# A two-layer graph kernel: owner matrices turned on TensorE, limits compared on GpSimd, and a new order of issue

## Chip, cores and metric

The kernel runs on one core of one Trainium2 chip. The metric is device time in microseconds (us) of one execution, the median over runs; lower is better. The core has five engines that run beside each other: TensorE (PE in the profile, with its weight loads as PEld), VectorE (DVE), ScalarE (ACT), GpSimd (POOL) and SyncE (SP, which here only issues transfers). Each engine works through its own instructions strictly in the order in which the program issues them, and waits on semaphores for the others.

## The reference, cut to what matters

There are 128 graphs (B) of 128 nodes (N) with 64 features (F). Layer 0 has 192 hidden units (H). Its sum over neighbours of a relu of a pair is the costly part:

```
mask = (adj > 0)
h  = relu(x@W1a [j] + (x[j]-x[k])@W1b + b1)        # for every pair j,k
hm = einsum('bjkh,bjk->bjh', h, mask)
x  = layernorm(x + hm@W2 + deg*b2)                 # layer 0
m  = relu(relu(x@W1+b1)@W2+b2);  msg = relu(adj@m)
r,z,n = gates(msg@W_ih, x@W_hh)                    # a GRU cell
x  = layernorm(x + (1-z)*n + z*x)                  # layer 1
```

Roughly one pair in eight is an edge (an edge is drawn with a mean chance of 0.0625 in each direction and then made symmetric), and some nodes have many more than others. The kernel therefore does not compute all pairs: for each node it gathers the projected rows of its neighbours, one neighbour slot after another.

## The kernel before, in words

The graphs are worked on in 32 groups of four (G = 4). A group passes through parts, each a Python generator whose steps issue a few instructions:

- `load`: transfers of `adjT`, `xT` and `x`. All go through SP's queue; `adjT` and `xT` of group 0 go through ACT's.
- `masks`, `ranks`, `degrees`, `counts`: a 0/1 mask (GpSimd, L422), the rank of each neighbour by a triangular product (L429, copied to `rankT`, L432), the degrees (L437 to L442), and the number of extra segments of each node (`nseg`, GpSimd, L447 to L455).
- `offsets` (L458 to L478): where each node's extra segments begin. Two small products (`po`, L462), ACT copies one of them as `woff` (L465), VectorE compares a ramp with the other one straight from PSUM, which gives `till` (L470, one instruction of 128x512), TensorE turns `till` into the owner matrix `pp` (L473), and ACT copies that twice, as `own` (bf16, L476) and `own32` (f32, L478).
- `turned` (L487): `rankT` transposed by a DMA on SP's queue. `owners` (L493): `own` transposed in the same way into `ownTh`, which ACT widens to `ownT` (f32, L498). `places` (L500): the slot numbers of extra segments.
- `pick0`, `pick1`: 0/1 selection matrices, made on VectorE (L518, L532, L540). `pieces` and `values0`: the two projections (L547), one of them split into three bf16 pieces b0, b1, b2 (ACT L574, TensorE L577).
- `seed0`, `gather0`, `keep0`, `reduce`: the first neighbour slots of every node. ACT seeds a PSUM tile `pv` (L606), TensorE adds twelve products of selections and pieces (L636; one such gather is "x12" in the profile), ACT applies the first relu (L656) and VectorE adds the others (L666). `gather0[i,k]` stands below for graph i and step k. `over0`, `over2` (`pz`, L617, copied as `us`, L623), `seed1`, `gather1`, `keep1`, `reduce1` do the same for the extra segments of nodes with many neighbours.
- `base`, `together`, `joined` (GpSimd, L686 to L699) and `sums` (`ph`, L711 to L730) add everything up into `hmT`.
- `second` (L286): layer 0's last product (`pw`, L290 and L294), the sum `y` (VectorE, L298), and a layernorm: statistics on VectorE (L260, L262), four short steps on GpSimd (L265 to L271), and four ACT instructions that write `x1` (L275). `turn` transposes `x1` (`pt`, L305, copied as `x1T`, L309). Then come `message1` to `message3` (`pm`, `pn`, `pa`), `gates` (`pg`) and `update`, which ends in a second layernorm and the store.

Two pools of PSUM are shared by all parts: three tiles for `pv` and the pieces, and two tiles for everything else (`pc`, `pd`, `po`, `pp`, `ps`, `pu`, `pz`, `ph`, `pw`, `pt`, `pm`, `pn`, `pa`, `pg`), so that a product waits until the tile two places earlier has been read.

The order of all work is written out by hand. `TIMETABLE` gives each step of each part a key; group g's step has the key plus g times 100,000, and the program issues all steps of all groups in the order of their keys. So in the steady state every 100,000 keys make a period, in which each part of some group is issued once, and a key's last five digits (after adding 100,000 until it is positive) give its place in the period. `FIRST` and `SETUP` replace the keys of group 0 and of the constants, and the last group is finished in two halves of two graphs (parts named `_a` for the half that holds graphs 0 and 1). In this last group `filler(n)` issues n products of zeros on TensorE between the steps of its tail.

Of the kernel before, what the change touches and what calls it, by code (L numbers as in the profile page):

```python
# [8 lines left out]
F32 = mybir.dt.float32  # L9
BF16 = mybir.dt.bfloat16  # L10
I32 = mybir.dt.int32
AF = mybir.ActivationFunctionType
ALU = mybir.AluOpType
AX = mybir.AxisListType

N = 128
# [3 lines left out]
G = 4  # L20
# [8 lines left out]

PER = 100000  # L30
TIMETABLE = {
    "load": (-374155,), "masks": (-371858,), "ranks": (-359377, -359144), "degrees": (-369319, -367849),
    "turned": (-272568, -171369), "counts": (-333387,), "offsets": (-310900, -305943, -303488, -292051, -285534),
    "owners": (-153741, -131732), "places": (-270818, -268534),
    "pieces": (-333718, -314824, -313814, -310191, -307850, -307567, -306941, -306158, -304141, -301647, -297445),
    "others": (-209792, -151063), "values0": (-277700, -277635, -275480),
    "pick0": (-320732, -302387, -282581, -212470), "pick1": (-264046, -174794), "over0": (-187960, -184290),
    "over2": (-185520, -182217), "base0": (-167649,), "base1": (-162372,), "base2": (-164467,), "base3": (-167914,),
    "together0": (-192391, -176074, -152715), "sums0": (-135068, -121634, -119241, -112824), "joined0": (-123048,),
    "joined2": (-118176,), "together1": (-152595, -149638, -144598), "together2": (-138498, -136957, -119891),  # L40
    "sums2": (-106974, -105339, -103492, -102357), "together3": (-118393, -118393, -118207),
    "second": (-101830, -101830, -95538, -87073, -83594, -80961), "turn": (-71249, -69447),
    "message1": (-68165, -67985), "message2": (-66138, -64498), "message3": (-64168, -63125),
    "gates": (-61275, -60655, -60562, -60317, -60317, -59857),
    "update": (-28741, -17657, -15933, 2994, 5175, 17014, 40040, 59482, 73748),
    "second_a": (-111100, -110015, -107069, -106567, -103378, -99663), "turn_a": (-92426, -81714),
    "message1_a": (-77007, -70724), "message2_a": (-67059, -65898), "message3_a": (-64395, -63864),
    "gates_a": (-2585, 1906, 7556, 8397, 14259, 14787),
    "update_a": (31311, 98242, 403034, 540592, 1029378, 1397305, 1422534, 2329328, 3382657),
    "seed0": (-239029, -208652, -204666, -193414, -193414, -184279, -167332, -163359),  # L50
    "gather0": (-236595, -215481, -206970, -203094, -202533, -193838, -186392, -183598, -181405, -172481, -169740,
        -166341, -163928, -161205, -159527, -145074), "keep0": (-218713, -195286, -179448, -161724),
    "reduce": (-209107, -203867, -196740, -190891, -186219, -180588, -169406, -168830, -166160, -161020, -158388,
        -143709), "seed1": (-174669, -161027),
    "gather1": (-170052, -167751, -164502, -162019, -160643, -157628, -136154, -128967), "keep1": (-168203, -159725),
    "reduce1": (-166795, -164060, -161924, -149299, -134445, -118338),
}


LAST = ("second_a", "turn_a", "message1_a", "message2_a", "message3_a", "gates_a", "update_a")  # L60
SETUP = (-385974, -327363, -291126, -281259, -225667, -75165)
FIRST = {
    "load": (-287111, -272305), "masks": (-279478,), "ranks": (-272173, -266612), "degrees": (-258449, -257828),
    "turned": (-188322, -105244), "counts": (-244130,), "offsets": (-216625, -212945, -212777, -205972, -195707),
    "places": (-185210, -182042),
    "pieces": (-270553, -265591, -263742, -257675, -254043, -249305, -246306, -243488, -243290, -240054, -221265),
    "values0": (-244645, -244472, -237344), "pick0": (-236759, -233220, -233160, -207088),
    "pick1": (-177321, -171760), "over0": (-195488, -187431),
}


# [1 line left out]
def adj_resnorm_kernel(  # L73
# [19 lines left out]
    nc = tc.nc  # L93
# [6 lines left out]
    ident_h = const.tile([N, N], BF16, name="ident_h")  # L100
# [13 lines left out]
    iota = const.tile([N, N], BF16, name="iota")  # L114
# [24 lines left out]
    def each(t, n):  # L139

        return t.rearrange("p (o c) -> p o c", o=1).to_broadcast([t.shape[0], n, t.shape[1]])
# [95 lines left out]
    def wide(t, n, w=F):  # L237
        return t.rearrange("p (g o) -> p g o", o=1).to_broadcast([N, n, w])
# [10 lines left out]
    def tail_parts(g, work, ps_w, n, store, lo=0, fill=True):  # L249

        name = g["name"]
        s = {}
# [26 lines left out]
        def filler(n):  # L279

            if fill and name == str(ng - 1):
                p = g["spare"]
                for i in range(n):
                    nc.tensor.matmul(p, ones_h, zeros, start=True, stop=True)

        def second():  # L286
            ps = [ps_w.tile([N, n // 2, F], F32, tag="w", name=f"pw{name}") for h in range(2)]
            hm = g["hmT"]
            for i in range(n):
                nc.tensor.matmul(ps[i % 2][:, i // 2, :], hm[:, (lo + i) // 2, i % 2, :], w2c[:, 0, :], start=i < 2, stop=False)  # L290
            yield
            for i in range(n):
                hs = slice(i % 2 * F, (i % 2 + 1) * F)
                nc.tensor.matmul(ps[i % 2][:, i // 2, :], hm[hs, (lo + i) // 2, 2, :], w2c[hs, 1, :], start=False, stop=i >= n - 2)  # L294
            yield
            y = work.tile([N, n, F], F32, tag="y0", name=f"y0_{name}")
            for h in range(2):
                nc.vector.tensor_add(y[:, h:n:2, :], ps[h], g["t4"][:, lo + h : lo + n : 2, :])  # L298
            filler(9)
            yield from layernorm(y, "0", "x1")  # L300

        def turn():
# [87 lines left out]
    with ExitStack() as fast:  # L390
        loads = fast.enter_context(tc.tile_pool(name="loads", bufs=4))
        prep = fast.enter_context(tc.tile_pool(name="prep", bufs=2))
# [3 lines left out]
        ps_w = fast.enter_context(tc.tile_pool(name="ps_w", bufs=2, space=bass.MemoryType.PSUM))  # L396

        def loading(s):
            def part():
                g = s["g"]  # L400
                gs = slice(g * G, (g + 1) * G)
                s["adjT"] = loads.tile([N, G, N], F32, tag="adjT", name=f"adjT{g}")
                q = nc.scalar if g == 0 else nc.sync
                q.dma_start(s["adjT"], adjT[:, gs, :])
                if g == 0:
                    yield

                s["xT"] = loads.tile([N, 2, N], F32, tag="xT", name=f"xT{g}")
                for h in range(2):
                    q.dma_start(s["xT"][h * F : (h + 1) * F], xT[:, g * G + h : (g + 1) * G : 2, :])  # L410
                s["x"] = loads.tile([N, G, F], F32, tag="x", name=f"x{g}")
                nc.sync.dma_start(s["x"], x[:, gs, :])
                yield

            return part

        def prep_parts(s):
            g = s["g"]
# [39 lines left out]
            def offsets():  # L458

                p = ps_w.tile([N, 2, G], F32, tag="w", name=f"po{g}")  # L460
                for c, m in enumerate((strict, incl)):
                    nc.tensor.matmul(p[:, c, :], m, s["nseg"], start=True, stop=True)  # L462
                yield
                s["woff"] = prep.tile([N, G], BF16, tag="woff", name=f"woff{g}")
                nc.scalar.mul(s["woff"], p[:, 0, :], 2.0 * W1)  # L465
                yield


                s["till"] = prep.tile([N, G, N], BF16, tag="till", name=f"till{g}")
                nc.vector.tensor_tensor(s["till"], each(iota, G), wide(p[:, 1, :], G, N), ALU.is_lt)  # L470
                yield
                p = s["po"] = ps_w.tile([N, G, N], F32, tag="w", name=f"pp{g}")
                nc.tensor.matmul(p, step, s["till"], start=True, stop=True)  # L473
                yield
                s["own"] = prep.tile([N, G, N], BF16, tag="own", name=f"own{g}")
                nc.scalar.copy(s["own"], s["po"])  # L476
                s["own32"] = prep.tile([N, G, N], F32, tag="own32", name=f"own32_{g}")
                nc.scalar.copy(s["own32"], s["po"])  # L478
# [12 lines left out]
                yield  # L491

            def owners():  # L493
                t = prep.tile([N, G, N], BF16, tag="ownTh", name=f"ownTh{g}", bufs=1)
                nc.sync.dma_start_transpose(t, s["own"].rearrange("p g n -> p (g n)"))
                yield
                s["ownT"] = prep.tile([N, G, N], F32, tag="ownT", name=f"ownT{g}")
                nc.scalar.copy(s["ownT"], t)  # L498

            def places():  # L500

# [245 lines left out]
        name, g, run = "setup", -1, setup(ps_g, ps_w)  # L747
# [153 lines left out]
```

## Time and profile before

| what | value |
|---|---|
| time, median of 3 runs | 963.09 us (959.31 to 966.01) |
| the profiled execution's own time | 966.28 us |
| its span, first to last instruction | 964.5 us, granted clock of TensorE 0.988 |
| busy TensorE, VectorE, ScalarE, GpSimd | 899.8, 861.4, 834.4, 771.6 us |
| chain that ended last, by engine | PE 53%, ACT 25%, DVE 16%, issue 5% |
| first gather of group 0 | starts at 17.04 us |
| last add of the last group (L666) | ends at 936.61 us |

A line of a timeline gives start, duration, engine, source line, operation, tile written from tiles read, shape and count; neighbouring instructions of one kind are merged, and idle time ahead of it stands in brackets with what ended it. A line of a table by stretches gives, for each engine, its busy time and its number of instructions. Products on TensorE overlap, so that the time from one line's start to the next one's start says more than the duration in the line.

### The profile page before, as it was taken

How to read it: one execution, taken by the hardware profiler on the slowest of the kernel's cores; microseconds unless marked ns; L12 is line 12 of the kernel's file. 1: busy time of each engine (PE TensorE's matmuls, PEld its weight loads, DVE VectorE, ACT ScalarE, POOL GpSimd, SP SyncE). 2: the span in 40 equal slices, each digit the busy share in tenths (PEclk: the TensorE clock that was granted, in tenths of full speed). 3: DMA queues.
4: the chain of work that ended last, by engine and by line, in shares of the span. 5: the costliest groups of instructions: out<-in, count | busy, mean ns of one | idle time of the engine just before them, and what ended most of it. 6: DMA issues, size and time to landing. Idle time of an engine off the chain costs nothing.

```text
span 964.5 us, 32114 instructions
## 1 busy us (share of the span) xinstructions
PE 899.8 (93%) x13081; PEld 711.2 (74%) x13084; DVE 861.4 (89%) x1628; ACT 834.4 (87%) x1705; POOL 771.6 (80%) x1113
## 2 busy tenths in 40 slices
PE   6889999999999999999999999999999999999984
PEld 3667777777777777777777777777777777777762
DVE  7898999999999999999999999999999999999772
ACT  4778889999989989988999898998998899989763
POOL 4548888888988888988888898888898888888663
PEclk9999999999999999999999999999999999999997
DMA  3101110012111012111012111102111201110000
GB/s 104 46 3 33 40 40 19 24 40 40 41 40 33 10 41 40 40 40 39 11 32 40 40 40 41 30 12 40 39 41 40 41 9 34 40 40 19 13 7 14
DMA packets 60523, 32.27 MB, mean 33 GB/s; under 512 B 38989, under 2 KB 56275, under 8 KB 60371
## 3 DMA queue, kind: packets, MB, share of 16 engines
q1 hardware_dynamic: 59938, 29.78, 12.8%
q8 instruction: 104, 1.70, 0.7%
q10 hardware_dynamic: 432, 0.39, 0.1%
q14 instruction: 49, 0.39, 0.1%
HBM read 17.57 MB, written 4.19 MB: 23 GB/s over the span
## 4 chain that ended last, share of the span: by engine, by line
PE 53%; ACT 25%; DVE 16%; issue 5%; POOL 1%; ACTq 0%; DVEq 0%; POOLq 0%
PE pv L636 25%; DVE acc L666 10%; ACT pv L606 7%; PE ph L718 4%; ACT x L275 3%; PE pw L290 3%; PE pv L547 3%; ACT acc L656 3%; ACT b L574 3%; ACT us L623 3%; PE ph L724 2%; PE pw L294 2%; DVE n L362 2%; ACT own L476 2%; PE pm L313 2%
## 5 line engine op out<-in xcount | busy, mean ns | idle before, releaser
L666 DVE SCALAR_TENSOR_TENSOR acc<-pv,acc 128x768 f32<-128x768 f32 x576 | 536.2, 949 | 62.4 <-PE pv L636 46.7
L636 PE MATMUL pv<-b,pick 64*128 64x192 bf16 x9216 | 476.8, 244 | 42.3 <-DVE acc L666 17.0
L636 PEld LDWEIGHTS <-pick 64*128 64x128 bf16 x9216 | 383.8, 95 | 130.0 <-issue 106.0
L606 ACT COPY pv<-u 128x768 f32<-128x768 f32 x256 | 204.7, 805 | 2.8 <-DVE acc L666 2.1
L656 ACT ACTIVATE acc<-pv 128x768 f32<-128x768 f32 x192 | 154.1, 803 | 14.2 <-PE pv L636 11.4
L691 POOL TENSOR_TENSOR fs<-acc,nb 128x192 f32<-128x192 f32 x128 | 76.4, 597 | 106.2 <-ACT nb L678 101.3
L686 POOL TENSOR_TENSOR acc<-acc 128x384 f32<-128x384 f32 x128 | 128.0, 1000 | 25.3 <-DVE acc L666 25.3
L688 POOL TENSOR_TENSOR acc<-acc 128x192 f32<-128x192 f32 x128 | 130.7, 1021 | 5.1
L518 DVE TENSOR_TENSOR pick<-rankT,ramp 128x2048 bf16<-128x2048 bf16 x64 | 91.5, 1432 | 0.0
L574 ACT CAST b<-pv 128x384 bf16<-128x384 f32 x192 | 83.0, 487 | 9.1 <-PE pv L547 3.0
L269 POOL TENSOR_TENSOR rs<-ve,nhalf 128x4 f32<-128x4 f32 (+1 forms) x66 | 86.1, 1305 | 0.0
L699 POOL TENSOR_TENSOR acc<-acc 128x384 f32<-128x384 f32 x64 | 78.0, 1219 | 0.5 <-DVE acc L666 0.5
L606 ACT COPY pv<-us 128x768 f32<-128x768 f32 x64 | 51.9, 811 | 24.5 <-DVE acc L666 24.5
L730 ACT COPY hmT<-ph 128x384 f32<-128x384 f32 x64 | 30.6, 478 | 36.9 <-PE ph L724 36.9
L617 PE MATMUL pz<-u,own 128*128 128x192 f32 x256 | 58.3, 350 | 0.2 <-ACT us L623 0.2
L532 DVE TENSOR_TENSOR pick<-pick 128x1024 bf16<-128x1024 bf16 x64 | 56.4, 882 | 0.0
L678 ACT ACTIVATE nb<-u,npad 128x192 f32<-128x192 f32 x128 | 53.8, 445 | 0.0
L422 POOL TENSOR_SCALAR maskT<-adjT 128x512 bf16<-128x512 f32 x32 | 48.3, 1510 | 4.4 <-DMA adjT<-in_adjT_dram 4.4
L376 POOL TENSOR_TENSOR uc<-ub,tn 128x256 f32<-128x256 f32 x31 | 51.1, 1648 | 0.0
L275 ACT ACTIVATE o<-y,nm,rs 128x64 f32<-128x64 f32 x128 | 45.7, 429 | 2.7 <-POOL nm L271 2.7
L617 PEld LDWEIGHTS pz<-u,own 128*128 128x128 f32 x256 | 39.8, 189 | 9.4 <-ACT own L478 4.9
L275 ACT ACTIVATE x<-y,nm,rs 128x64 f32<-128x64 f32 x128 | 46.0, 432 | 0.0
(142 smaller groups left out, 1540.2 us busy)
## 6 DMA issues: line engine op xcount, KB each, us to landing
adjT<-in_adjT_dram SPq DMA_DIRECT2D x31, 256.0 KB, 3.0
x<-in_x_dram SPq DMA_DIRECT2D x32, 128.0 KB, 2.6
xT<-in_xT_dram SPq DMA_DIRECT2D x62, 64.0 KB, 2.8
out_dram<-o SPq DMA_DIRECT2D x31, 128.0 KB, 1.7
rank<-rankT SPq DMA_TRANSPOSE x32, 2.7
ownTh<-own SPq DMA_TRANSPOSE x32, 2.3
adjT<-in_adjT_dram ACTq DMA_DIRECT2D x1, 256.0 KB
wab<-in_w_dram SPq DMA_DIRECT2D x2, 96.0 KB, 3.2
```

The lines of the kernel that those rows point to most:

```text
L269: nc.gpsimd.tensor_tensor(rs, ve, nhalf[:, 0:n], ALU.pow)
L275: nc.scalar.activation(s[into][:, i, :], y[:, i, :], AF.Identity, bias=nm[:, i : i + 1], scale=rs[:, i : i + 1])
L518: nc.vector.tensor_tensor(s[name][:, rows], s[src].rearrange("p (o g) n -> p o g n", o=1).to_broadcast([N, n, G, N]), ramp[:, first : firs ...
L574: nc.scalar.copy(b[c][:, h::2, :], ps[h])
L606: nc.scalar.copy(v, src.to_broadcast(list(v.shape)))
L617: nc.tensor.matmul(p[:, i, :], s["own32"][:, i0 + i, :], s["u"][:, i0 + i, :], start=True, stop=True)
L636: nc.tensor.matmul(v[:, h, j, :], pick[ks], s[f"b{c}"][ks, gr, :], start=False, stop=c == 2, skip_group_check=True,)
L656: nc.scalar.activation(kept(s, t, i), view(s["pv", t, i, 0]), AF.Relu)
L666: nc.vector.scalar_tensor_tensor(out=a, in0=view(s["pv", t, i, k // CH if t == 0 else 0]), scalar=0.0, in1=a, op0=ALU.max, op1=ALU.add,)
L686: nc.gpsimd.tensor_tensor(f[:, 0], f[:, 0], f[:, 1], ALU.add)
L688: nc.gpsimd.tensor_tensor(f[:, 0, 0], f[:, 0, 0], f[:, 0, 1], ALU.add)
L699: nc.gpsimd.tensor_tensor(f[:, 0], f[:, 0], f[:, 1], ALU.add)
```

## The change

Five things are changed.

1. `owners` no longer goes through a DMA. TensorE transposes the four 128x128 bf16 matrices of `own` into a new PSUM tile `pq` of the shared pool, and ACT copies that as `ownT`.
2. `till` is no longer one VectorE instruction of 128x512 but four GpSimd instructions of 128x128, each against a limit in a column of `off`, which ACT copies from PSUM ahead of `woff`.
3. For group 0, `xT` is named directly behind `adjT` on ACT's queue; only `x` comes in the second step of `load`.
4. `filler(9)` in `second` becomes `filler(2)`.
5. All keys are new: `TIMETABLE`, `SETUP` and `FIRST`.

```
     def second():
-            filler(9)
+            filler(2)
...
     def loading(s): def part():
                 q.dma_start(s["adjT"], adjT[:, gs, :])
-                if g == 0:
-                    yield
                 s["xT"] = loads.tile([N, 2, N], F32, tag="xT", name=f"xT{g}")
                 for h in range(2):
                     q.dma_start(s["xT"][h * F : (h + 1) * F], xT[:, g * G + h : (g + 1) * G : 2, :])
+                if g == 0:
+                    yield
                 s["x"] = loads.tile([N, G, F], F32, tag="x", name=f"x{g}")
...
     def offsets():
+                off = prep.tile([N, G], F32, tag="off", name=f"off{g}")
+                nc.scalar.copy(off, p[:, 1, :])
                 s["woff"] = prep.tile([N, G], BF16, tag="woff", name=f"woff{g}")
                 nc.scalar.mul(s["woff"], p[:, 0, :], 2.0 * W1)
                 yield
                 s["till"] = prep.tile([N, G, N], BF16, tag="till", name=f"till{g}")
-                nc.vector.tensor_tensor(s["till"], each(iota, G), wide(p[:, 1, :], G, N), ALU.is_lt)
+                for i in range(G):
+                    nc.gpsimd.tensor_scalar(s["till"][:, i, :], iota, off[:, i : i + 1], None, ALU.is_lt)
...
     def owners():
-                t = prep.tile([N, G, N], BF16, tag="ownTh", name=f"ownTh{g}", bufs=1)
-                nc.sync.dma_start_transpose(t, s["own"].rearrange("p g n -> p (g n)"))
+                p = ps_w.tile([N, G, N], BF16, tag="w", name=f"pq{g}")
+                for i in range(G):
+                    nc.tensor.transpose(p[:, i, :], s["own"][:, i, :], ident_h)
                 yield
                 s["ownT"] = prep.tile([N, G, N], F32, tag="ownT", name=f"ownT{g}")
-                nc.scalar.copy(s["ownT"], t)
+                nc.scalar.copy(s["ownT"], p)
```

Of the new keys, those of the stretch around `second` and `turn`, of GpSimd's steps ahead of it, and of the transfers:

```
-    "turned": (-272568, -171369), "offsets": (-310900, -305943, -303488, -292051, -285534),
+    "turned": (-206152, -150702), "offsets": (-250979, -238779, -227252, -221365, -215957),
-    "owners": (-153741, -131732),
+    "owners": (-56871, -54418),
-    "others": (-209792, -151063), "over0": (-187960, -184290), "over2": (-185520, -182217),
+    "others": (-127608, -124864), "over0": (-113155, -112899), "over2": (-119901, -114573),
-    "second": (-101830, -101830, -95538, -87073, -83594, -80961), "turn": (-71249, -69447),
+    "second": (-25475, -23201, -23201, -19183, -16525, -11604), "turn": (-10715, -7388),
-    "values0": (-277700, -277635, -275480),
+    "values0": (-196023, -193451, -192607),
-    "joined2": (-118176,),
+    "joined2": (-31891,),
-    "second_a": (-111100, -110015, -107069, -106567, -103378, -99663), "turn_a": (-92426, -81714),
+    "second_a": (-19096, -19096, -18328, -13331, 2255, 18603), "turn_a": (38564, 44760),
```

Read modulo 100,000, TensorE's work between `second`'s last products (`pw`, L294) and `turn`'s transposes (`pt`) is in order:

- before: gather0[1,1], `pp`, `pz` (over0), gather0[1,2], `pz` (over2), gather0[1,3], gather0[2,0], `pu` (values0), gather0[2,1], then `pt`;
- after: gather0[1,1], `pp`, `pz` (over2), gather0[1,2], `pz` (over0), gather0[1,3], gather0[2,0], then `pt`.

GpSimd's work ahead of the layernorm of `second` is in order, after the change: `joined2`, the first step of `others`, the four compares of `till`, the second step of `others`, the first step of `together0`, then the layernorm's steps (L265 to L271). In the last group the second half's `pt`, `pm`, `pn`, `pa`, `pg` all come behind the first half's `pg`; before, the two halves alternated.

## The prediction

> **What bounds the kernel now.** I read the page's busy times first, then a table by stretches for the period, then the timelines of each engine inside one period, then the head and the tail. The 36-product run of TensorE starts at 134.97 us and, 26 groups later, at 876.65 us: the period is 741.68 / 26 = 28.53 us, and 31 of them make most of the span. In one such stretch:
>
> ```profile
> 449.00:477.50 28.50, 27.48 (x412) 21.91 (x410) 26.47 (x50) 25.92 (x54) 24.23 (x35) 1.00 0.14 35
> ```
>
> The columns are PE, PEld, DVE, ACT, POOL. TensorE idles 28.53 - 27.48 = 1.05 us a period, VectorE 2.1, ScalarE 2.6, GpSimd 4.3; DMA is at 0.14. TensorE is the bound, and what remains of its idle time are short waits in an order that hides nearly everything. The stretch in which the change alters most:
>
> ```profile
> 458.86 0.66 PE L294 MATMUL pw<-w2c,hmT 64*128 64x64 f32 x8
> 459.36 0.66 PE L636 MATMUL pv<-b,pick 64*128 64x192 bf16 x12
> 459.97 0.38 PE L473 MATMUL pp<-till,step 128*128 128x512 bf16 x1
> 460.18 0.90 PE L617 MATMUL pz<-u,own 128*128 128x192 f32 x4
> 461.02 0.67 PE L636 MATMUL pv<-b,pick 64*128 64x192 bf16 x12
> 461.62 0.92 PE L617 MATMUL pz<-u,own 128*128 128x192 f32 x4
> 462.89 1.17 PE L636 MATMUL pv<-b,pick 64*128 64x192 bf16 x24 [0.36 <-DVE acc L666]
> 463.88 0.86 PE L547 MATMUL pu<-wall,xT 64*128 64x192 f32 x8
> 464.56 0.34 PE L557 MATMUL pu<-three,ones_h 64*128 64x384 bf16 x2
> 465.12 0.67 PE L636 MATMUL pv<-b,pick 64*128 64x192 bf16 x12 [0.23 <-ACT acc L656]
> 465.73 0.44 PE L305 MATMUL pt<-ident,x 128*128 128x128 f32 x2
> ```
>
> TensorE has 6.87 us (458.86 to 465.73) of work and small waits between pw's second half and pt. In that time pw must become x1:
>
> ```profile
> 459.62 0.49 DVE L298 TENSOR_TENSOR y<-pw,t 128x128 f32<-128x128 f32 x2 [0.18 <-PE pw L294]
> 460.54 0.36 DVE L262 BATCH_NORM_AGGREGATE mv<-stats 128x2 f32<-128x6 f32 x4
> ```
>
> ```profile
> 461.01 0.23 POOL L265 TENSOR_SCALAR ve<-mv 128x4 f32<-128x4 f32 x1
> 461.50 1.03 POOL L269 TENSOR_TENSOR rs<-ve,nhalf 128x4 f32<-128x4 f32 x1
> 462.62 0.20 POOL L271 TENSOR_TENSOR nm<-nm,rs 128x4 f32<-128x4 f32 x1
> ```
>
> ```profile
> 462.94 1.43 ACT L275 ACTIVATE x<-y,nm,rs 128x64 f32<-128x64 f32 x4
> ```
>
> x1 is complete at 464.37, so this chain takes 464.37 - 458.86 = 5.51 us, and pt finds it 1.36 us early.
>
> **The change, part by part.**
>
> *Owners on TensorE.* The nearest row is the run of `ps` (L508 and L511), bf16 128x128 with a new weight each, whose starts lie 0.055 us apart (466.21, 466.27, 466.33): 4 x 0.055 = 0.22 us a period on the bound. From below it is 0 (all of it falls into idle time), from above 4 x 0.098 us, the weight load of L511, = 0.39. I take 0.22, as the row is the same shape. ACT's copy was 0.62 us from SBUF; from PSUM the row is `own` (L476), 0.59: nothing. SP loses a transpose of 1.20 us of issue. SP waits 23 us a period for the store's input, so that buys nothing. The store, the next load and the rank transpose still stand behind one another on SP; in the new order the store sits 53% of a period, 15 us, ahead of `places`, against 2.7 us of landing. The shared pool gets a 20th tile a period: pq waits for the last gate read and is read 1 to 2 us later, with gathers in between.
>
> *Limits on GpSimd.* VectorE loses 0.68 us (L470) a period, but it idles 2.1 us already and waits for TensorE (1.2 us in this window), so I cost the relief itself at nothing (a tenth of a us comes back below). ACT gains `off`, 0.20 us by `woff` (L465), within 2.6 us of idle time. GpSimd has no such row:
>
> ```profile
> L422 POOL TENSOR_SCALAR maskT<-adjT 128x512 bf16<-128x512 f32 x32 | 48.3, 1510 | 4.4 <-DMA adjT<-in_adjT_dram 4.4
> L470 DVE TENSOR_TENSOR till<-iota,po 128x512 bf16<-128x512 bf16 x32 | 21.7, 679 | 4.1 <-ACT woff L465 4.1
> ```
>
> From the mask's 1.51 us for 512 columns and 0.23 us for 4 (L265), a 128-column compare is 0.23 + 124 x 1.28 / 508 = 0.54 us, four are 2.2. From below 4 x 0.23 = 0.9, from above 4 x 0.60 (the longest part of 128x192, L691) = 2.4. I take 2.2: same operation and output type. GpSimd rises to 26.4 of its period and stays below TensorE; its idle cover falls from 4.3 to about 2.
>
> A rule speaks against this step: the Trainium skill, "GPSIMD Engine Reference", section "Performance versus the Vector engine", holds GpSimd to be about half as fast as VectorE elementwise. By that the compares would cost 2 x 0.68 = 1.4 us (an estimate from that page and L470); by the rows it is 2.2, and neither fills GpSimd's idle time.
>
> What stands behind the compares on GpSimd matters more: t4, together0's first sum, then ve, which starts x1's chain. GpSimd is also slowed by VectorE at times: `uc` (L376) has a median of 1.71 us and `y` (L379), of the same shape, 0.73; at 457.46 uc runs beside a pick of 1.53 us (L518). The skill's "SBUF — State Buffer", section "SBUF: two separate sides", calls the port of the two an exclusive lock; the 1 us here fits. In the new order pick1 (1.28) and its subtraction (0.94) run beside the compares. I take no loss from it (the sum ahead of ve starts when VectorE is done with pick1), and keep up to 1 us a period for the range.
>
> *The new order.* Between pw's second half and pt there is now: rest of pw 0.50, gather 0.61, pp 0.21, pz 0.84, gather 0.60, pz 0.91, two gathers 0.99 (each from start to next start above) = 4.66 us. pu (1.24) and a gather are now behind pt. The chain still takes 5.51 us. So TensorE must stand still for at least 5.51 - 4.66 = 0.85 us there, where it stood for 0.36 + 0.23 = 0.59. ACT's order adds: x1 stands behind the copy of the second pz, which itself waits for the copies of pp, and gets off some 0 to 0.4 us later. I take 0.90 us, near the floor, as ACT's queue has 2.6 us of idle time. Behind the waiting pt stand places, pm and the next four gathers, and behind these all adds: nothing catches up, as TensorE is the bound. The other idle time of a period (1.05 - 0.59 = 0.46) can go from 0 (all gone) to 1.0 (GpSimd late); I take 0.36, a tenth less than now, since a wait that ends with VectorE ends earlier when VectorE has 0.68 us less to do.
>
> Period: 27.48 + 0.22 + 0.90 + 0.36 = 28.96 us, or 31 x (28.96 - 28.53) = +13.3 us.
>
> *First xT.* xT of group 0 is issued on ACT at 5.44, just after the mask ended (5.33), and pieces' products wait for it (2.56 us before 8.53, and again to 9.75). Named behind adjT it goes out at once; the products can start when the weights are ready (7.2). But the first gather also needs values0, whose bias waits for VectorE's `three`; its 2.8 us (7.52 to 10.34) now stand behind pick0's first compare, which waits for rankT, at about 11. So gather 0 starts near 17 as before: 0, from -2.2 to +2.
>
> *Tail.* The fillers hold TensorE from 943.70 to 946.48; with two, x1 of the second half comes at 945.85 in place of 946.79: -0.95. In the new order hmT's second half no longer waits behind the first half's layernorm: last add to y was 6.78 us (936.61 to 943.39) and becomes 4.4 to 5.1 (joined 1.0, ph 1.5, hmT 0.5, pw 1.1 to 1.8, hops). But pt to pg of the two halves, interleaved until now, run one after the other: one is 4.3 us (947.61 to 951.9), and two output layernorms (1.43 each, L275) get in front on ACT. 4.7 + 3.3 + 8.6 + 1.4 + 10.1 = 28.1 against 27.9. With fewer fillers the clock is low for longer (pw takes 1.12 at 941.62 and 0.66 at 937.20), 0 to 2 us. I take +0.8.
>
> Sum: 13.3 + 0 + 0.8 = +14.1, 966.28 + 14.1 = 980.4 for the profiled execution. That one lies 3.2 above the median, so 977.
>
> **Rivals.**
> 1. *The bound absorbs it (not slower).* If all idle time outside the stretch goes, the period is 27.48 + 0.22 + 0.85 = 28.55, and the time 963.09 + 31 x 0.02 = 964. It decides when fewer than 0.3 us of other waits remain: 31 x 0.32 is 1%. For it: VectorE has 0.68 us less to do, and two of TensorE's three waits end with VectorE or ACT. Against it: those waits are order, not load.
> 2. *GpSimd is late.* If compares and locks delay ve and joined2 by 1 us a period, it is 30.1 and 963 + 31 x 1.6 = 1013. For it: only 2 us of cover are left. Against it: GpSimd waits 2.8 us a period for nb today, slack that can be used.
> 3. *Faster.* The head's 2.2 us, the filler, and an order that starts x1's chain earlier than I count (pw back to back with y, no stall at pt): 27.7 + 0.4 = 28.1, 963 - 13 - 3 = 947. Against it: the chain's 5.51 us are rows, not queues.
>
> **How the numbers follow.** My forecast (973 to 1002) 0.50; rival 1 (954 to 973) 0.32; rival 2 (above 1002) 0.10; rival 3 (below 953.5) 0.08. Within 1% is 953.5 to 972.7, about what a measurement of this kernel can tell from no change. So faster 0.08, same 0.32, slower 0.50 + 0.10 = 0.60. The range 959 to 1002 leaves out rivals 2 and 3 and the lowest part of rival 1.
>
> **What would show it.** After: a period near 29.0; a wait of TensorE at pt (L305) or its weight load, put down to x1 (L275), of 0.5 to 1 us in each period; compares of 0.5 us on GpSimd; VectorE below 26.0 us a period; first gather at 17. If pt does not wait, the stretch was misread; if the period is right but the waits end with GpSimd's joined or compares, rival 2's mechanism holds in small.

## The result, and the profile after

The changed kernel takes 970.81 us (median of 7 runs, 969.89 to 971.96); the kernel before, beside it, 962.14 us (7 runs, 959.31 to 966.01). The ratio is 1.0089 (95% interval 1.0070 to 1.0108): 0.9% slower, just inside the 1% that was set as the limit of what can be told from no change by time alone, though the interval excludes 1. The profiled execution took 971.44 us, its span is 969.7.

The page of the changed kernel, its busy times and the shares of the chain that ended last:

```profile
PE 899.1 (93%) x13203; PEld 715.1 (74%) x13205; DVE 838.2 (86%) x1596; ACT 826.8 (85%) x1737; POOL 856.6 (88%) x1241
...
POOL 39%; DVE 24%; PE 21%; ACT 8%; issue 8%; DVEq 0%; ACTq 0%; POOLq 0%
```

In the kernel before the same chain was PE 53%, ACT 25%, DVE 16%. TensorE's busy share has hardly moved; what ends last has. The period, taken from the first 64-row product with w2 (pw's second half, L292) at 434.28 to that at 862.51, 15 groups later, is 28.55 us; before, by the same measure, it was 28.52. One period in the table by stretches (PE, PEld, DVE, ACT, POOL):

```profile
449.00:477.55 28.55, 27.38 (x416) 22.05 (x414) 25.77 (x49) 25.64 (x55) 26.83 (x39) 1.00 0.17 30
```

VectorE lost 0.70 us, GpSimd gained 2.60 and is now the engine with most work after TensorE. The stretch that the prediction built its sum on, TensorE's timeline from pw's second half to pt:

```profile
462.83 0.66 PE L292 MATMUL pw<-w2c,hmT 64*128 64x64 f32 x8
...
465.72 0.92 PE L618 MATMUL pz<-u,own 128*128 128x192 f32 x4
466.99 1.17 PE L637 MATMUL pv<-b,pick 64*128 64x192 bf16 x24 [0.36 <-DVE acc L667]
468.09 0.78 PE L303 MATMUL pt<-ident,x 128*128 128x128 f32 x2
468.70 0.38 PE L505 MATMUL ps<-strict_w,ones_h 128*128 128x512 bf16 x1
```

The work in it is as forecast, and so is its length: from pw's second half to ps it takes 5.87 us (462.83 to 468.70). pt's two products now stretch over 0.61 us up to ps (465.73 to 466.00, or 0.27, before), because the second's weights, x1, come late. GpSimd and VectorE around the same time, two timelines of the changed kernel:

```profile
459.20 3.10 POOL L470 TENSOR_SCALAR till<-iota,off 128x128 bf16<-128x128 bf16 x4
...
462.96 1.71 POOL L687 TENSOR_TENSOR acc<-acc 128x384 f32<-128x384 f32 x1
465.10 0.23 POOL L263 TENSOR_SCALAR ve<-mv 128x4 f32<-128x4 f32 x1 [0.42 <-DVE mv L260]
```

```profile
459.60 0.96 DVE L667 SCALAR_TENSOR_TENSOR acc<-pv,acc 128x768 f32<-128x768 f32 x1 [2.13 <-PE pv L637]
460.48 1.36 DVE L519 TENSOR_TENSOR pick<-place,ramp 128x2048 bf16<-128x2048 bf16 x1
461.76 0.95 DVE L667 SCALAR_TENSOR_TENSOR acc<-pv,acc 128x768 f32<-128x768 f32 x1
462.62 1.19 DVE L541 TENSOR_TENSOR pick<-pick 128x1536 bf16<-128x1536 bf16 x1
...
468.76 0.95 DVE L667 SCALAR_TENSOR_TENSOR acc<-pv,acc 128x768 f32<-128x768 f32 x1
```

Four compares take 3.10 us here, and ve still waits 0.42 us for VectorE: GpSimd gets there early. The chain that ended last, in one turn of the steady part, says what does hold it:

```profile
461.76 0.95 DVE acc L667
462.70 0.84 DVE pick L541
...
464.07 0.40 PE pp L473
...
464.50 0.59 ACT own L476
...
465.98 0.96 DVE acc L667
...
467.73 1.11 DVE pick L519
468.83 0.88 DVE acc L667
...
469.78 1.92 POOL acc L687
...
485.66 0.61 POOL fs L692
486.26 0.04 issue
486.31 0.44 PE ph L712 x2
...
487.44 0.62 PE pv L637 x12
...
488.15 0.96 DVE acc L667
...
490.31 0.94 DVE acc L667
```

It starts with an add of VectorE at 461.76 and comes back to the same add at 490.31, 28.55 us later: a closed loop, one period long. From 469.78 to 486.26, 16.5 us, GpSimd works through its queue with no pause over 0.1 us (together, the layernorms' steps, the mask, counts); its last sum feeds three transposes (ph, L712) on TensorE; behind these in TensorE's order stands a gather; VectorE's add waits for that gather (the 2.13 us above); and GpSimd's sum waits for VectorE's adds. The detour of this chain through `pp` and ScalarE's copies (464.07 to 465.98) is not needed for that: VectorE's own timeline has no pause from 459.60 to 469.71. So one turn is 10.1 us of VectorE's queue, 16.5 of GpSimd's and 1.9 of TensorE's (486.26 to 488.15, the add of 459.60 one period later). No engine is full. The order itself closes the loop. The four compares are not in it: they run from 459.20, just after the part of GpSimd's queue that is.

The loop says why the period is 28.55 and not less. It does not say why the changed kernel is slower than the one before: the two periods differ by 0.03 us, under 1 us over all groups.

Where the 5.2 us between the two profiled spans (969.7 - 964.5) arise, read from the starts of pw's second half: group 0 at 57.97 (54.67 before), +3.3; group 2 at +3.0; group 29 at 891.06 (886.66), +4.4; end +5.2. So some 3 in the head, 1.4 in the steady part, and 0.8 after group 29. The medians differ by 8.7, as the profiled execution of before lies 4.1 above its median, that of after 0.6; the 3.5 us between 5.2 and 8.7 are not explained by these traces.

In the head, VectorE's timeline and TensorE's:

```profile
10.75 1.22 DVE L519 TENSOR_TENSOR pick<-rankT,ramp 128x2048 bf16<-128x2048 bf16 x1 [2.75 <-ACT rankT L429]
...
12.05 0.25 DVE L144 CAST piece<-bias 128x192 bf16<-128x192 f32 x1
```

```profile
6.66 2.71 PE L548 MATMUL pv<-wall,xT 64*128 64x192 f32 x8 [1.97 <-DVE wall L203]
...
19.08 1.14 PE L637 MATMUL pv<-b,pick 64*128 64x192 bf16 x12 [0.25 <-ACT pv L607]
```

xT is no longer waited for: the projected products start at 6.66 in place of 8.53. But the bias pieces (L144) start at 12.05, against 7.52 before, behind a compare for which VectorE waits 2.75 us, and the first gather starts at 19.08, against 17.04.

### The profile page after: what moved, and what is told of

Its sections match the earlier page's. It is cut to its first block, busy times and chain, and to the rows that moved or that the text cites. A ratio compares the mean times of both kernels' runs of the same rounds, so it can differ in the third digit from the quotient of the medians.

```text
span 969.7 us, 32418 instructions
## 1 busy us (share of the span) xinstructions
PE 899.1 (93%) x13203; PEld 715.1 (74%) x13205; DVE 838.2 (86%) x1596; ACT 826.8 (85%) x1737; POOL 856.6 (88%) x1241
## 3 DMA queue, kind: packets, MB, share of 16 engines
q8 instruction: 105, 1.72, 0.8%
## 4 chain that ended last, share of the span: by engine, by line
POOL 39%; DVE 24%; PE 21%; ACT 8%; issue 8%; DVEq 0%; ACTq 0%; POOLq 0%
DVE acc L667 12%; POOL acc L687 11%; PE pv L637 8%; POOL fs L692 6%; POOL acc L689 5%; DVE pick L519 4%; POOL acc L700 4%; POOL maskT L419 4%; POOL rs L267 3%; DVE pick L541 2%; ACT own L476 2%; POOL uc L374 2%; POOL y L377 2%; PE ph L712 2%; DVE stats L258 2%
## 5 line engine op out<-in xcount | busy, mean ns | idle before, releaser
L637 PE MATMUL pv<-b,pick 64*128 64x192 bf16 x9216 | 462.8, 244 | 24.2 <-DVE acc L667 14.6
L637 PEld LDWEIGHTS <-pick 64*128 64x128 bf16 x9216 | 380.0, 95 | 92.4 <-issue 71.5
L687 POOL TENSOR_TENSOR acc<-acc 128x384 f32<-128x384 f32 x128 | 185.3, 1448 | 37.4 <-DVE acc L667 37.3
L607 ACT COPY pv<-u 128x768 f32<-128x768 f32 x256 | 205.8, 814 | 0.4 <-DVE acc L667 0.4
L657 ACT ACTIVATE acc<-pv 128x768 f32<-128x768 f32 x192 | 155.2, 809 | 24.8 <-PE pv L637 24.4
L575 ACT CAST b<-pv 128x384 bf16<-128x384 f32 x192 | 85.9, 483 | 26.1 <-PE pv L578 15.5
L470 POOL TENSOR_SCALAR till<-iota,off 128x128 bf16<-128x128 bf16 x128 | 98.8, 789 | 2.3 <-ACT off L462 2.3
L700 POOL TENSOR_TENSOR acc<-acc 128x384 f32<-128x384 f32 x64 | 77.5, 1211 | 7.0 <-DVE acc L667 6.0
L519 DVE TENSOR_TENSOR pick<-rankT,ramp 128x2048 bf16<-128x2048 bf16 x64 | 77.7, 1214 | 2.8 <-ACT rankT L429 2.8
L689 POOL TENSOR_TENSOR acc<-acc 128x192 f32<-128x192 f32 x128 | 76.9, 601 | 2.7
L607 ACT COPY pv<-us 128x768 f32<-128x768 f32 x64 | 51.4, 803 | 20.7 <-DVE acc L667 20.6
L267 POOL TENSOR_TENSOR rs<-ve,nhalf 128x4 f32<-128x4 f32 (+1 forms) x66 | 67.4, 1022 | 0.0
L533 DVE TENSOR_TENSOR pick<-pick 128x1024 bf16<-128x1024 bf16 x64 | 59.7, 932 | 0.0
L371 POOL TENSOR_TENSOR ub<-ua,rz 128x256 f32<-128x256 f32 x31 | 50.5, 1630 | 2.4
```

The costliest lines, as they stand in the source:

```text
L267: nc.gpsimd.tensor_tensor(rs, ve, nhalf[:, 0:n], ALU.pow)
L470: nc.gpsimd.tensor_scalar(s["till"][:, i, :], iota, off[:, i : i + 1], None, ALU.is_lt)
L519: nc.vector.tensor_tensor(s[name][:, rows], s[src].rearrange("p (o g) n -> p o g n", o=1).to_broadcast([N, n, G, N]), ramp[:, first : firs ...
L607: nc.scalar.copy(v, src.to_broadcast(list(v.shape)))
L637: nc.tensor.matmul(v[:, h, j, :], pick[ks], s[f"b{c}"][ks, gr, :], start=False, stop=c == 2, skip_group_check=True,)
L657: nc.scalar.activation(kept(s, t, i), view(s["pv", t, i, 0]), AF.Relu)
```

## The experiments

Every run is compared with the kernel before on the same chip (its median was 961.5 to 962.1 in the three sets of runs). The changed kernel itself stands at a ratio of 1.0089. "Period" is between starts of pw's second half over 15 groups of the steady part, "tail" from the end of VectorE's last add to the end of the span, both of the profiled execution.

| kernel | us | ratio to before, 95% | period | tail |
|---|---|---|---|---|
| before | 962.14 | 1 | 28.52 | 27.9 |
| changed | 970.81 | 1.0089 (1.0070 to 1.0108) | 28.55 | 28.9 |
| changed, limits on VectorE | 977.60 | 1.0175 (1.0158 to 1.0192) | 28.75 | 29.9 |
| changed, five compares | 981.89 | 1.0209 (1.0193 to 1.0226) | 28.93 | 29.4 |
| changed, eight transposes | 967.79 | 1.0067 (1.0053 to 1.0081) | 28.41 | 28.8 |
| changed, pt later | 981.59 | 1.0210 (1.0196 to 1.0224) | 28.84 | 29.9 |
| before + all parts | 1031.08 | 1.0694 (1.0669 to 1.0720) | 30.80 | 27.0 |
| before + limits on GpSimd | 1029.76 | 1.0689 (1.0663 to 1.0714) | 30.79 | 24.3 |
| changed, ph behind the gather | 964.07 | 1.0014 (1.0002 to 1.0026) | 28.23 | 29.3 |
| changed, limits in VectorE's wait | 967.76 | 1.0053 (1.0033 to 1.0073) | 28.41 | 29.9 |
| changed, bias pieces first | 970.04 | 1.0088 (1.0071 to 1.0105) | 28.55 | 28.9 |
| before + owners on TensorE | 966.35 | 1.0043 (1.0030 to 1.0057) | 28.67 | 25.5 |
| changed, three mends | 970.98 | 1.0092 (1.0077 to 1.0107) | 28.25 | 37.2 |
| the same, limits in VectorE's wait | 970.81 | 1.0085 (1.0069 to 1.0100) | 28.27 | 36.2 |

**Limits on VectorE.** The first theory was that GpSimd, idle for only 1.7 us a period, had become the bound; the rival, that TensorE still was, through pt.

```
-                for i in range(G):
-                    nc.gpsimd.tensor_scalar(s["till"][:, i, :], iota, off[:, i : i + 1], None, ALU.is_lt)
+                nc.vector.tensor_tensor(s["till"], each(iota, G), wide(off, G, N), ALU.is_lt)
```

> The changed kernel with one thing undone: till is again one VectorE instruction of 128x512, at the place in the order where the four GpSimd compares stood; its limits come from the copy off, so ScalarE's work is unchanged. GpSimd loses 3.1 us of its 26.8 a period, VectorE gains 0.7 on its 25.8. If GpSimd has become the bound (its idle time in the changed kernel is 1.7 us a period, most of it hand-offs of 0.07 us), the period falls from 28.55 to about 28.2, TensorE's 27.4 plus its remaining waits: 11 us less, 960 us. If TensorE and its wait at pt still set the period, it stays within 0.1 and the time at 968 to 973.

Both missed, on the other side: 977.60, 6.8 us more than the changed kernel, with 3 us less work on GpSimd in each period. VectorE's timeline shows where the compare went:

```profile
462.72 0.96 DVE L666 SCALAR_TENSOR_TENSOR acc<-pv,acc 128x768 f32<-128x768 f32 x1 [2.14 <-PE pv L636]
463.59 0.68 DVE L469 TENSOR_TENSOR till<-iota,off 128x512 bf16<-128x512 bf16 x1
464.19 1.22 DVE L518 TENSOR_TENSOR pick<-place,ramp 128x2048 bf16<-128x2048 bf16 x1
```

It stands between the add that waits and the pick, inside the loop, and the period grew by 0.20. GpSimd's load does not set the period, then; its place in the loop does.

**Five compares** (the first done twice).

```
-                for i in range(G):
+                for i in (0, 0, 1, 2, 3):
                     nc.gpsimd.tensor_scalar(s["till"][:, i, :], iota, off[:, i : i + 1], None, ALU.is_lt)
```

> The changed kernel with the first of the four compares issued twice (the same values are written again), so that GpSimd has one more instruction of 0.6 us in each period, the same place. GpSimd theory: it has no slack ahead of the layernorm's steps, so the period grows by 0.5 to 0.8 us, 987 to 996 us. TensorE theory: the 1.7 us of GpSimd's idle time take it, 971 to 975 us.

981.89: 0.38 us a period for a compare of 0.61 (the median), between the two. The compares stand beside the loop with the 0.42 us that ve waits as their only margin, and a fifth uses it up: ve (471.94) now follows GpSimd's sum without a pause. In some early groups the compares become part of the chain that ended last (3.97 us of `till` in one piece, at 146.63). In the steady part they do not. What is longer there is a pick of VectorE on the loop: 1.72 us at 473.81, against 1.19 at 467.65 in the changed kernel. It starts 0.08 us after GpSimd's `ua` (473.73), which used to be done by then. That this is the whole of the 0.38 is read from the lines and was not tried.

**Eight transposes** (the four of the owners done twice).

```
-                for i in range(G):
+                for i in (0, 1, 2, 3, 0, 1, 2, 3):
                     nc.tensor.transpose(p[:, i, :], s["own"][:, i, :], ident_h)
```

> The changed kernel with the four transposes of own issued twice into the same tile, so that TensorE has 4 x 0.055 = 0.22 us more in each period (estimate from the spacing of bf16 128x128 products). TensorE theory: 31 x 0.22 = 7 us more, 977 us. GpSimd theory: TensorE idles 1.2 us a period and takes them in, 970 to 973 us.

967.79, 3 us less than with four. TensorE's own load is not what sets the changed kernel's period. The loop is gone from the chain that ended last, which is PE 59%, DVE 21%, ACT 15% and POOL 0% here, against POOL 39% in the changed kernel. That more work made it faster by 0.14 us a period fits a loop through two engines that slow each other (the 128x384 sums, L687, fell from 1448 to 1312 ns on average, being shifted against VectorE's picks), but why the shift helps was not tried by itself.

**pt later.** pt and pm were moved behind the next gathers, so that TensorE needn't wait for x1.

```
-"turn": (-10715, -7388), "message1": (-5853, -5792)
+"turn": (-5700, -5690), "message1": (-4530, -4150)
```

> The changed kernel with only keys moved: pt (the transposes of x1) goes behind places and gather0[2,1], and pm and its copy move back behind the next gather, so that TensorE has about 1.3 us more work between pw and pt. My prediction's step was that TensorE loses its time by waiting for x1 at pt: if so, the wait of about 0.4 us a period goes and the time falls by 8 to 12 us, to 960. GpSimd theory: the wait goes, another takes its place, and the time stays within 3 us of 971.

981.59, slower by 10.8 than the changed kernel; no theory had it. The wait did go. The line of pt's weight load (idle time ended by x1: us in total, times), in the changed kernel and here:

```profile
  ACT x L273: 13.6, 33
```

```profile
  ACT x L273: 4.1, 2
```

But pm comes late now. ScalarE stands 0.6 us a period at its copy (m, L315), with seeds and keeps queued behind it, and TensorE's gathers wait for those: 0.37 us a period for a seed (L607), 0.31 for a keep (L657). That chain's share is PE 68%. The wait at pt was the cheaper one.

**All parts in the old order, and the limits alone.** Both keep the old timetable's keys; the first takes all four edits of the code, the second only the four compares and the copy of the offsets.

```
 TIMETABLE, SETUP, FIRST of the kernel before
+                off = prep.tile([N, G], F32, tag="off", name=f"off{g}")
+                nc.scalar.copy(off, p[:, 1, :])
...
-                nc.vector.tensor_tensor(s["till"], each(iota, G), wide(p[:, 1, :], G, N), ALU.is_lt)
+                for i in range(G):
+                    nc.gpsimd.tensor_scalar(s["till"][:, i, :], iota, off[:, i : i + 1], None, ALU.is_lt)
```

> The kernel before with every part of the change except the new order: owners turned by TensorE, limits compared by GpSimd from a copy on ScalarE, xT loaded right behind adjT, two spare products at the end; all keys of the old timetable kept. Theory of the order (the 9 us of the change come from the new sequence, whose period is set by a loop through GpSimd's queue and VectorE's, and from the first gather 2 us later): 957 to 964 us, ratio to before 0.995 to 1.003. Theory of the parts (transposes on the engine that bounds, compares on a busy GpSimd): 967 to 973, with a period of 28.7 or more.

> The kernel before with only the limits moved: four compares on GpSimd and the copy of the offsets on ScalarE, old timetable. GpSimd idled 4 us of each 28.5 in the kernel before, 2.8 of it in one wait. Theory that GpSimd's work is hidden as long as that wait is left: 959 to 964. Theory that the compares by themselves delay what GpSimd hands on: 966 to 975.

All ranges were far off: 1031.08 and 1029.76, 7% slower. The limits alone do it. GpSimd's timeline with the limits alone:

```profile
489.19 2.36 POOL L473 TENSOR_SCALAR till<-iota,off 128x128 bf16<-128x128 bf16 x4
...
493.01 1.00 POOL L689 TENSOR_TENSOR acc<-acc 128x384 f32<-128x384 f32 x1
494.10 0.23 POOL L265 TENSOR_SCALAR ve<-mv 128x4 f32<-128x4 f32 x1
```

In the old order there is no pause ahead of ve (in the kernel before neither: the sum ahead of it ends at 460.93, ve starts at 461.01), and x1, ScalarE's adds and TensorE's gathers follow from it; the period grew by 2.27 us, nearly the whole 2.36 of the compares. The chain that ended last closes on itself here too, with the compares on it: from GpSimd's `acc` (L702) at 484.75 through `till`, ve, x1, ScalarE, TensorE and VectorE back to the same `acc` at 515.53, 30.78 us later. GpSimd still idles 2.7 us in each period at fs, waiting for ScalarE's nb: slack in another place, which pays for nothing here. So the part that was costed at nothing costs 68 us in the old order, and the new order is what hides it.

**ph behind the gather.** If the loop is the cause, cutting it at one edge is enough: the transposes that wait for GpSimd's last sum go behind the gather that VectorE waits for.

```
-"sums2": (-38501, -31584, -30196, -30196)
+"sums2": (-36999, -31584, -30196, -30196)
```

> The changed kernel with one step of TensorE's order moved: the three transposes of fs that wait for GpSimd's last sum (61499) stand behind the gather that VectorE waits for (63000), no longer ahead of it. Theory of the loop (VectorE's add waits for a gather queued behind these transposes, which wait for GpSimd's sums, which wait for VectorE's adds; one turn is one period): the turn shortens by about 0.65 us until TensorE bounds again, a period of 28.2 to 28.45, 961 to 968. Theory that GpSimd's own load of 26.8 us sets the period: 28.55 stays, 969 to 972. Theory that hmT, 0.6 us later, now holds the product with w2: slower, 973 to 980.

964.07 (12 runs, 962.60 to 965.25), 6.7 us less than the changed kernel, the period 28.23. One step moved by one place on one queue, nothing added or removed. The theory of the loop holds, the two others fall. One part of its forecast is not shown, that TensorE bounds again: TensorE still idles 0.95 us a period, and the chain that ended last is PE 32%, POOL 29%, ACT 19% and DVE 16%, so what sets 28.23 stays open. The period in the table by stretches:

```profile
432.10:460.33 28.23, 27.28 (x413) 22.06 (x412) 25.60 (x49) 25.55 (x55) 26.74 (x39) 1.00 0.17 30
```

**Limits in VectorE's wait.** As in the first run, but the compare goes ahead of the add, into the wait.

```
-"offsets": (-250979, -238779, -227252, -221365, -215957)
+"offsets": (-250979, -238779, -228000, -221365, -215957)
```

> The changed kernel with the limits compared by one VectorE instruction, as in the first run of this study, but placed one add earlier (key 72000 in place of 72748), into VectorE's wait of 2.1 us for a gather. Theory of the loop (in that first run the compare stood between two adds inside the loop and lengthened it by 0.2 us a period; GpSimd's compares stand beside it): the period falls back to 28.5 to 28.55, 968 to 972, though GpSimd has 3 us less to do. Theory that GpSimd's load binds: 28.4 or less, 960 to 966. Theory that VectorE's load binds: 977 again.

967.76, 9.8 us less than with the same instruction one add later:

```profile
454.64 0.84 DVE L469 TENSOR_TENSOR till<-iota,off 128x512 bf16<-128x512 bf16 x1
456.84 0.96 DVE L666 SCALAR_TENSOR_TENSOR acc<-pv,acc 128x768 f32<-128x768 f32 x1 [1.35 <-PE pv L636]
```

The period is 28.41, 0.1 below what the loop alone was to give, and above what GpSimd's load was to give. VectorE's load is excluded as the bound; between the other two the time does not decide by itself. The trace does more. GpSimd is busy for 24.2 us a period here and still has 43% of the chain that ended last, with nearly the same part of its queue in one piece, 16.4 us (466.88 to 483.3); so it is the place of its work that counts. And the two picks beside which no compares run any more (457.71 and 459.71) take 1.22 and 0.95 us in place of 1.36 and 1.19, which shortens VectorE's part of the loop; a wait of 0.17 us for pw takes some of it back.

**Bias pieces first.**

```
-SETUP = (-214889, -204507, -202221, -178353, -154861, -11337)
+SETUP = (-214889, -204507, -202221, -190000, -154861, -11337)
```

> The changed kernel with one step of the setup moved ahead: the pieces of the bias on VectorE (-178353) stand before the first group's first compare (-189573) again, as in the kernel before. Theory that this order costs the head its 2 us (first gather at 19.1 us against 17.0 before): first gather near 17, time 967.5 to 969.5. Theory that the head is held elsewhere (GpSimd's four compares before the first product of them, group 1's loads queued ahead of the weights on SP): within 1 us of the changed kernel, 970 to 971.5.

The trace says yes in part: the first gather starts at 17.77 (19.08 in the changed kernel), group 1's pw at 89.2 (91.4), and the span is 2.3 shorter. The time says 970.04 against 970.81, which is within the intervals. So the order of the pieces holds part of the head, and whether it is worth 2 us in the time is open. The pieces start 1.9 us later than in the kernel before, as the load of the bias itself now stands behind group 1's loads on SP; VectorE's timeline:

```profile
9.44 0.26 DVE L144 CAST piece<-bias 128x192 bf16<-128x192 f32 x1 [1.94 <-DMA bias<-in_b_dram]
```

**Owners on TensorE alone.**

```
-                t = prep.tile([N, G, N], BF16, tag="ownTh", name=f"ownTh{g}", bufs=1)
-                nc.sync.dma_start_transpose(t, s["own"].rearrange("p g n -> p (g n)"))
+                p = ps_w.tile([N, G, N], BF16, tag="w", name=f"pq{g}")
+                for i in range(G):
+                    nc.tensor.transpose(p[:, i, :], s["own"][:, i, :], ident_h)
```

> The kernel before with only the owners' transpose on TensorE (four transposes and a copy from PSUM, no DMA). The prediction's term: 0.22 us a period on the engine that bounds, 968 to 969.5 (bounds 0 to 0.39: 961 to 974). Theory that the transposes fill TensorE's gaps, as four more of them did in the changed kernel: 960 to 964.

966.35, +4.4 us (from 961.96) or 0.14 a period: between the two. In the old order, where TensorE does bound, four transposes cost about what their starts' distances say.

**Three mends together, without and with the limits on VectorE.** ph behind the gather, the bias pieces first, and the last group's halves alternating again (keys of `second_a` to `update_a` set among those of the second half).

> The changed kernel with three mends: fs's transposes behind the gather (964.1 by itself), the bias pieces first in the head, and the two halves of the last group alternating in the tail. If they add up: 964.1 less 2 for the head, less 1 to 2 for the tail, 959.5 to 962, at or just below the kernel before. If the head's mend is taken back by the next wait and the tail's halves wait for each other: 963 to 966.

> The run beside it (all three mends), with the limits also compared by one VectorE instruction in its wait for the gather, so that GpSimd keeps 3 us less. Theory that TensorE bounds once the loop is cut (28.2): within 1.5 us of the run beside it. Theory that what GpSimd hands on still sets a part of the period: 3 to 6 us below it. Theory that VectorE's wait is used up (1.6 us left of it, and a compare of 0.7): 3 to 8 us above it.

970.98 and 970.81: 7 us more than with the first mend alone. The steady part and the head did as expected (period 28.25; the last add ends at 932.07, against 933.40 with ph's move alone). All the loss is in the tail, 37.2 us in place of 29.3: that mend was wrong. The two runs agree within 0.2 us, so once the loop is cut, 3 us of GpSimd's work change nothing.

## Why the prediction was partly right

The time, 970.8, lies in the range, 6 below the forecast of 977 and 7 above the 964 of rival 1; it is in rival 1's band (954 to 973), not in that of the likeliest case (973 to 1002). The sum was +14.1, the two profiled spans show +5.2, and its terms were further off than that.

- **The period, 27.48 + 0.22 + 0.90 + 0.36 = 28.96, or +13.3 us: this is the step that failed.** Measured: 28.55, busy 27.38 and idle 1.17, +1.4 us over the steady part. The stretch from pw to pt was right in its sum: 4.66 of work, 0.90 of standing still and 0.27 of pt make 5.83 us, and it takes 5.87. Of the 0.94 that TensorE stands still there, 0.34 is at pt (0.61 - 0.27) and 0.36 ahead of a gather. The rest of the period was not: it was to be 23.13 (28.96 - 5.83) and is 22.68, with four more transposes in it. "Nothing catches up, as TensorE is the bound" is the sentence that fails. The step took TensorE's 27.48 for a load that stays whatever the order, and its waits for something to add to that. But the same work on TensorE is 27.66 us busy with the owners alone in the old order, 27.38 in the changed kernel and 27.28 with ph moved, and taking the wait at pt away made things slower. The runs show a loop in its place: eight transposes in place of four were faster, and one reordered edge of the loop gave 6.7 us. Rival 1's number (28.55) was right, its reason (TensorE's bound absorbs the rest) was not.
- **Owners, +0.22 a period (0 to 0.39).** In the old order +0.14, a fair size. In the new order four more of them cost nothing.
- **Limits at nothing, GpSimd below TensorE.** The cover was named wrongly: GpSimd's idle time as a sum. In the old order the step by itself costs 2.27 us a period. It is hidden only where the new order puts it, with 0.42 us to spare, and not wholly: with one VectorE instruction in the wait in its place the period is 0.14 shorter. The compare was put at 0.54 us; where no pick runs beside it, it takes 0.60, the upper bound. So four cost 2.4 us against 0.68 on VectorE, 3.5 times as much, which the Trainium skill's factor of two ("GPSIMD Engine Reference", section "Performance versus the Vector engine") undershoots further.
- **No loss from the shared port.** In sum this held, at the place that counts it did not. The sums of 128x384 take longer in the new order, where they run beside picks; those of 128x192 take less. The two groups in the kernel before and in the changed one:

```profile
L686 POOL TENSOR_TENSOR acc<-acc 128x384 f32<-128x384 f32 x128 | 128.0, 1000 | 25.3 <-DVE acc L666 25.3
L688 POOL TENSOR_TENSOR acc<-acc 128x192 f32<-128x192 f32 x128 | 130.7, 1021 | 5.1
```

```profile
L687 POOL TENSOR_TENSOR acc<-acc 128x384 f32<-128x384 f32 x128 | 185.3, 1448 | 37.4 <-DVE acc L667 37.3
...
L689 POOL TENSOR_TENSOR acc<-acc 128x192 f32<-128x192 f32 x128 | 76.9, 601 | 2.7
```

  That is 4 x 0.45 = 1.8 us a period more and 4 x 0.42 = 1.7 less; without the compares GpSimd's busy time fell by 0.5 us a period (26.83 - 3.10 against 24.23). But the longer sums now lie on the loop: the one at the head of GpSimd's part (469.78) starts 0.16 us after a pick of 1.21 us (469.62) and takes 1.92, 0.92 more than it took before. This agrees with the exclusive lock that the Trainium skill describes ("SBUF — State Buffer", section "SBUF: two separate sides").
- **First xT, 0 (-2.2 to +2).** Mis-sized: +2.0 at the first gather and +3.0 to 3.4 at the first three groups' pw. The place was right (the bias pieces behind the first compare), but they come at 12.05, 4.5 us later than before, not 3.5. SP's order was not looked at: the bias itself is loaded behind group 1. It is the new keys that cost this, not xT: with all four edits and the old keys group 0's pw starts at 54.09, 0.6 ahead of the kernel before.
- **Tail, +0.8.** Measured +1.0 against the profiled execution of before (28.9 and 27.9). The filler's -0.95 was not seen. With all parts in the old order, and two spare products, the tail took 27.0 us; with the limits alone, and nine, 24.3. The granted clock (the third number from the end) was lower in the first. The 5 us behind the last add, with two and with nine:

```profile
1003.56:1008.56 5.00, 3.37 (x23) 2.56 (x21) 0.83 (x6) 1.32 (x4) 4.52 (x9) 0.75 0.01 2
```

```profile
1003.67:1008.67 5.00, 3.37 (x30) 2.69 (x29) 0.83 (x6) 1.73 (x4) 4.52 (x9) 1.00 0.00 2
```

  The number of spare products can't have started this fall. In stretches of half a microsecond the clock is at 0.50 from 1006.06 on, the spare products come only at 1009.92, and up to there TensorE's work is the same in both. The kernel before, with nine, fell too (0.71 in the same 5 us, 0.61 in the next, and a tail of 27.9); the owners alone, with nine, did not (25.5). Nine may bring the clock back sooner (it stays at 0.50 for about 7 us in the kernel before, for about 10 with two); that was not tried by itself. Nor does a low clock of its profiled execution explain why the kernel before is faster at the median: six other executions of it with the same mean clock, 0.988, took 961.5 to 962.2 us. Where those 3.5 us come from stays open.
- **Rival 2 (GpSimd late, 30.1 and 1013)** did not come true for the change, but its numbers come close to the old order with the compares (30.8 and 1030). That is in part luck: 1 us a period on top of 28.96 is 29.96 and not 30.1, and what the runs show is 2.3 on top of 28.5. **What would show it**: VectorE below 26.0 (25.77) and a wait in each period at pt for x1 came as named, the wait at 0.3 us and not 0.5 to 1; the period near 29.0, the compares of 0.5 and the first gather at 17 did not. "GpSimd's joined or compares" as the end of TensorE's waits was close: it is GpSimd's last sum, at ph.

No run beat the kernel before. The changed kernel with ph moved and the bias pieces first, but the last group as in the change, was not run; from 964.07 and the 0.8 us of time or 2.3 of span that the bias pieces gave, it would be at 962 to 963, an estimate: level with the kernel before.

## What to carry to other kernels

When every engine is 85 to 93% busy and the work is put in order by hand, follow the chain over one whole period and look whether it closes on itself: then the loop sets the period, and an edit is worth what it adds to the loop, not what it adds to the fullest engine. Idle time of an engine covers new work only if it lies at that place in its queue: here 2.7 us of it stood unused beside a loss of 2.3. A wait that can be seen (pt's) may be the cheapest place for time that has to go somewhere; look for the edge that holds up another engine's next step, and move that.

## What was not expected of the hardware

GpSimd's 128x384 sums take 0.99 us or, beside VectorE's bf16 picks, up to 1.99; a compare of 128x128 takes 0.60, up to 1.61. It goes the other way as well: a pick of 1.19 us took 1.72 when it started 0.08 us behind a GpSimd instruction of 0.73. In the 15 us behind the last add the granted TensorE clock fell to 0.50 for a time in all the traces with two spare products, but also in one of the three with nine, and in one pair it differed (0.75 and 1.00) while TensorE's busy time was the same, 3.37 us.
